# A state-space scan on one core: products issued ahead of their scans, named PSUM slots, and conv and projection pieces in other steps

## The chip, the cores and the metric

The kernel runs on one core of a Trainium2 chip. The time is device microseconds from the first to the last instruction of the program, as a median over runs. One execution was also recorded by the hardware profiler; all durations of instructions come from that one. The core has five engines that run their own instruction queues in order: TensorE (PE; its weight loads are listed as PEld), VectorE (DVE), ScalarE (ACT), GpSimd (POOL), and SyncE (SP), which here only issues DMAs.

## The reference

The input is 32 images of 96 channels and 56 x 56 pixels, all float32. Two layers follow one another:

- Layer 0 is a ConvNeXt block: a 7 x 7 depthwise convolution, a normalisation over channels, a product with w1 (96 to 384), GELU, a product with w2 (384 to 96), and the residual.
- Layer 1 reads the 3136 pixels of an image as a sequence and runs two Mamba blocks over it. Each block normalises, projects to x and z (192 channels each), applies a causal convolution of 4 taps and silu to x, computes from it `delta`, `B` and `C` (16 states), and then the recurrence, for each channel and each state,

```
h[t] = exp(delta[t] * A) * h[t-1] + delta[t] * B[t] * x[t]
y[t] = sum over states of C[t] * h[t]  + D * x[t]
```

  y is multiplied by silu(z), projected to 96 channels and added. After both blocks come a pooled branch, a fusing product, a batch normalisation over all images, and the residual.

## The kernel before, in words

**Tiling.** A sequence is cut into 4 chunks of 784 tokens, each in two halves of 392. A *stage* is one chunk of one image in one of the two Mamba blocks: 32 x 4 x 2 = 256 stages, in the list `stages`. Within a stage the 192 channels x 16 states are cut into 24 *steps*: group j (0 to 5) has 32 channels, quarter g (0 to 3) has 4 states, and a step works on 128 partitions (32 channels x 4 states) x 784 tokens. Step r of a stage has j = r // 4 and g = r % 4; n counts steps over all stages.

**A step.** It needs four things:

- `exps` (L869): ACT computes exp(delta * A). For an *unpooled* group (j = 0, 1, 3, 4) the result goes into an SBUF tile `da` (11 buffers), two steps ahead (`lead`, L882). For a *pooled* group (j = 2 and 5) it goes into PSUM, one step ahead.
- the product delta * x * B. For an unpooled group, `spread` (L886) has PE copy u = delta * x of 32 channels onto 128 partitions in a PSUM tile `u4` (two banks), and DVE multiplies by B just before the scan (L921), into a second PSUM tile `w`, or, for quarter 3, into `u4` in place. For a pooled group POOL multiplies instead (`pooled`, L899), in SBUF, from a copy of u that a DMA spread; those eight products of a stage are placed in steps 0, 2, 4, 6 and 12, 14, 16, 18.
- the scan on DVE (L928), which writes one of four slots of the ring `h`.
- the product with C on POOL (L932), into the `da` tile of the step. Three steps later PE sums this over states into the PSUM tile `y` (`add_up`, L948). After the second group of a pair, `gate` (L943) has DVE multiply y by silu(z). For steps 4 and 12 (`LATE`) the gate is issued between the product and the scan.

The slots for `u4`, `w` and the exponentials of pooled groups all come from one PSUM tag with two buffers of two banks (`wide`, L865).

**What runs beside it.** The order of every engine's instructions is that of the program; it is written by hand. Each piece of other work has a slot, a step number with a fraction: `put` (L973) files it and `run` issues all pieces of a step, by fraction, after the step's scan (those marked True in between, ahead of the scan). A slot below 0 or over 24 falls into a neighbouring stage. The pieces are:

- `prep` (L587): for the next stage, the normalisation (steps 11 to 15), the input projections (`project`, with the x weights in three thirds q = 0, 1, 2 from step 16 on, then `silu("xc")`, the z projections and `silu("z")`), `dbl` and `dt` (delta, B, C) and the DMAs that spread them. Its slots are the list `t` (L752), to which 0.1 is added.
- `post` (L784): output projection of the stage before, from step 7.5.
- `block0` (L400): half a chunk of layer 0 of a later image, steps 11 to 18, with `pool` and `fuse` once an image.
- `conv` (L534): the depthwise convolution of a pair of channels for 5 images, as products with a band matrix: two parts of 7 taps each (3 images and 2), each ended by ACT's copy and a DMA (`store`). There are 192 of them, one a stage.

All of these pieces use three PSUM tiles of one bank, `ps0`, `ps1`, `ps2` (`psum(k)`, L346). [...]

Of the kernel before, what the change touches and what calls it, by code (L numbers as in the profile page):

```python
# [34 lines left out]
F32 = mybir.dt.float32  # L35
I32 = mybir.dt.int32
AF = mybir.ActivationFunctionType
ALU = mybir.AluOpType
# [10 lines left out]
NG = 4  # L49
DTR = 6  # L50
NX = DTR + 2 * NS
NCH = 4
CH = L // NCH
HC = CH // 2
# [7 lines left out]
def convnext_mamba_kernel(  # L62
# [31 lines left out]
    nc = tc.nc  # L94
# [249 lines left out]
    with ExitStack() as main:  # L344
# [12 lines left out]
        def halves(t):  # L357
            return t.rearrange("p (a b) -> p a b", a=2)
# [41 lines left out]
        def block0(b, c, s):  # L400
            k = c * 2 + s
            v = {}

            def load():
                if k == 0:
                    batch_sums[b] = work([C, NCH * 2], "sums", 2)
                v["cv"] = work([C, ROWS, W], "cv", 1)
                g = 0 if b < b0 else 1 + (b - b0) // NB
                at = (b - groups[g][0]) * W
                nc.sync.dma_start(  # L410
                    v["cv"],
                    conv_d[g].rearrange("(c h) w -> c h w", h=H)[
                        :, k * ROWS : (k + 1) * ROWS, at : at + W
                    ],
                )

            def load_x():
                if s == 0:
                    xins[b, c] = work([C, CH], "xin", 1)
                    nc.sync.dma_start(xins[b, c], x[b, :, c * CH : (c + 1) * CH])  # L420

            def center():
                v["cv"] = v["cv"].rearrange("p r w -> p (r w)")
                v["ps"] = centred(v["cv"], 2)

            def square():
                v["sq"] = squared(v["ps"])

            def mean():
                v["ps"] = mean_of(v["sq"], 2)  # L430

            def root():
                if pre and s == 0:
                    exp_ln_tables()
                rsqrt(v["ps"])

            def norm():
                nc.vector.tensor_tensor(hn0s[s][0:C], v["cv"], v["ps"][0:C, 0:HC], ALU.mult)

            def up():  # L440
                v["pss"] = [psum(f) for f in range(NF)]
                for f in range(NF):
                    nc.tensor.matmul(
                        v["pss"][f][:, 0:HC], w1_sb[:, f * 128 : (f + 1) * 128], hn0s[s],
                        start=True, stop=True,
                    )

            def gelu():
                v["gl"] = work([128, NF, HC], "gl", 1)
                for f in range(NF):  # L450
                    nc.scalar.activation(
                        v["gl"][:, f], v["pss"][f][:, 0:HC], AF.Gelu, bias=b1_sb[:, f : f + 1]
                    )
                if not pre:
                    exp_ln_tables()

            def down():
                v["ps"] = psum(2)
                nc.tensor.matmul(
                    v["ps"][0:C, 0:HC], eye, xins[b, c][:, tok(s)], start=True, stop=False  # L460
                )
                for f in range(NF):
                    nc.tensor.matmul(
                        v["ps"][0:C, 0:HC], w2_sb[:, f, :], v["gl"][:, f, :],
                        start=False, stop=(f == NF - 1),
                    )

            def residual():
                xs = xins[b, c][:, tok(s)]
                nc.scalar.activation(  # L470
                    xs, v["ps"][0:C, 0:HC], AF.Identity, bias=b2ls,
                    accum_out=batch_sums[b][:, k : k + 1],
                )
                if s == 1:
                    nc.sync.dma_start(x1_d[b][:, c * CH : (c + 1) * CH], xins.pop((b, c)))


            def total():
                v["m"] = work([C, 1], "mean", 2)
                nc.vector.tensor_reduce(v["m"], batch_sums[b], AX.X, ALU.add)  # L480

            def pool():
                ps = psum(2)
                nc.tensor.matmul(ps[0:C, 0:1], gpw_sb, v["m"], start=True, stop=True)
                v["gp"] = work([C, 1], "gp", 2)
                nc.scalar.activation(v["gp"], ps[0:C, 0:1], AF.Relu, bias=gpb, scale=1.0 / L)

            def fuse():
                ps = psum(2)
                nc.tensor.matmul(ps[0:C, 0:1], fw2, v["gp"], start=True, stop=True)  # L490
                fb = (
                    const.tile([C, 1], F32, name="fb0")
                    if pre
                    else wp.tile([C, 1], F32, name="fb", tag="fb", bufs=3)
                )
                nc.scalar.activation(fb, ps[0:C, 0:1], AF.Identity, bias=fusb)
                batch_bias[b] = fb

            last = [(21.5, total), (29.9, pool), (30.9, fuse)] if k == 2 * NCH - 1 else []
            return last + [  # L500
                (-6, load), (2, load_x), (11.3, center), (12.1, square), (12.4, mean),
                (12.8, root), (14.1, True, norm), (15.6, up), (15.9, gelu), (17.3, down),
                (18.3, residual),
            ]
# [29 lines left out]
        def conv(g, p):  # L534
# [24 lines left out]
            def store(part):  # L559
# [11 lines left out]

                return piece

            at = (7.7, 8.2, 8.6, 9.2, 9.6, 10.2, 10.4), (18.5, 18.6, 19.2, 20.2, 21.2, 21.3, 22.2)
            return [
                (-1, load), (11.05, store(0)), (22.9, store(1)),
                *[(at[part][dw], tap(part, dw)) for part in range(2) for dw in range(7)],
            ]

# [7 lines left out]
        def prep(S):  # L587
# [161 lines left out]
                (-18, load), (-12.9, center), (-11.9, square), (-11.8, halo), (-11.6, mean),  # L749
                (-11.2, root), (-9, True, norm),  # L750
            ]
            t = (-7.6, -7.5, -6.5, -6, 0, 0.1, 1, 2.3, 3.1, 3.4, 4)  # L752
            if S in (stages[2], stages[-1]):

                start = [
# [106 lines left out]
        convs = [(g, p) for g in range(1, len(groups)) for p in range(C // 2)]  # L862
        halfs = [(b, c, s) for b in range(1, B) for c in range(NCH) for s in range(2)]

        def wide():  # L865

            return pu.tile([128, 1024], F32, name="w", tag="w", bufs=2)

        def exps(n):  # L869

            m, r = divmod(n, NSTEP)
            if m == len(stages):
                return
            S, j, g = stages[m], r // NG, r % NG
            if j in POOLED:
                e = wide()[:, 0:CH]
            else:
                e = S.da[j, g] = wp.tile([128, CH], F32, name="da", tag="da", bufs=11)
            nc.scalar.activation(e, S.d4[j], AF.Exp, scale=S.d["A"][:, j, g : g + 1])  # L879
            S.e[j, g] = e  # L880

        def lead(n):  # L882

            return 1 if n % NSTEP // NG in POOLED else 2

        def spread(n):  # L886

            m, r = divmod(n, NSTEP)
            if m == len(stages) or r // NG in POOLED:
                return  # L890
            S, j = stages[m], r // NG
            S.u4 = wide()
            for a in range(2):
                nc.tensor.matmul(  # L894
                    S.u4[:, 512 * a : 512 * a + HC], sel[rows(a), j % 2, :],
                    S.u[rows(a), j // 2, :], start=True, stop=True,
                )

        def pooled(m, j, g):  # L899


            def piece():
                S = stages[m]
                t = S.da[j, g] = wp.tile([128, CH], F32, name="da", tag="da", bufs=11)
                nc.gpsimd.tensor_tensor(t, S.us[j], S.bcs[g][:, 0, :], ALU.mult)  # L905

            return piece

        def scan(n):
            m, r = divmod(n, NSTEP)  # L910
            S, j, g = stages[m], r // NG, r % NG
            d, c = S.d, S.c
            da = S.da[j, g]
            if j in POOLED:
                db = da
            else:

                if g == 0:
                    S.w = wide()
                db = (S.u4 if g == NG - 1 else S.w)[:, 0:CH]  # L920
                nc.vector.tensor_tensor(  # L921
                    halves(db), S.u4.rearrange("p (a b) -> p a b", a=2)[:, :, 0:HC],
                    halves(S.bcs[g][:, 0, :]), ALU.mult,
                )
            if r in LATE and n >= NSTEP // 3:
                gate(n - LAG - 2)
            run(n, within)
            nc.vector.tensor_tensor_scan(  # L928
                ring[:, g, :], S.e.pop((j, g)), db, 0.0 if c == 0 else d["st"][:, j, g : g + 1],
                ALU.mult, ALU.add,  # L930
            )
            nc.gpsimd.tensor_tensor(da, ring[:, g, :], S.bcs[g][:, 1, :], ALU.mult)  # L932
# [54 lines left out]
        for m, S in enumerate(stages):  # L987
# [3 lines left out]
                put(m, [(NG * (j - 2) + 2 * g, pooled(m, j, g)) for g in range(NG)])  # L991
            if 2 <= m < len(halfs) + 2:
                put(m, block0(*halfs[m - 2]))
            if 2 <= m < len(convs) + 2:
                put(m, conv(*convs[m - 2]))
            if m + 1 < len(stages):
                put(m, prep(stages[m + 1]))
        put(len(stages), post(stages[-1]))
# [129 lines left out]
```

## Time and profile before

| | |
|---|---|
| median of 3 runs | 17278.04 us (17271.47 to 17292.32) |
| profiled execution, span | 17284.9 us |
| the program around the span | starts and ends with it: nothing is counted outside |
| stages | 559 to 16917 us; ahead of them weights and the first convolutions, after them the batch normalisation |
| one stage | 63.7 us (2259 scans between 3000 and 9000 us) |
| busy | DVE 93%, POOL 91%, PE 90%, ACT 66% |

A line of the profile's groups gives source line, engine, operation, what it writes and reads with shapes, how often, then the busy time in us and the mean of one in ns, and after the next bar the engine's idle time just before these instructions with what ended most of it. A line of the timeline gives start and length in us, and in brackets the engine's idle time before it. Ends of matmuls are modelled, so PE's busy time is not PE at its peak.

### The profile page before, as it was taken

To read this page: it belongs to the slowest core of one execution; us is meant where nothing else is said; L and a number is where in the kernel's file an instruction comes from. 1 tells how busy PE (TensorE), PEld (TensorE's weight loads), DVE (VectorE), ACT (ScalarE), POOL (GpSimd) and SP (SyncE) were. 2 spreads that over 40 slices of the span, in tenths; PEclk is the share of its full clock that TensorE was granted. 3 is DMA by queue.
4 is the path that set the end of the run, shared out by engine and by line. 5 is a ranking of instruction groups with operands and counts; after the bars stand their busy time and mean duration, and the time that the engine had idled before them with its cause. 6 is when DMAs were issued, how large, how long until landed. Compare 5 with 4: busy or idle time off the path is not lost. (4 is left out here: it accounts for less than half of the span.)

```text
span 17284.9 us, 207580 instructions
## 1 busy us (share of the span) xinstructions
PE 15488.9 (90%) x69336; PEld 5550.7 (32%) x69336; DVE 16068.6 (93%) x12351; ACT 11452.6 (66%) x18723; POOL 15673.1 (91%) x8798
## 2 busy tenths in 40 slices
PE   8899999999999999999999999999998888888870
PEld 5333333333333333333333333333332222222220
DVE  8699999999999999999999999999999999999994
ACT  1666676666666676666667667676666666666653
POOL 1699999999999999999999999999999999999991
PEclk9899999999999999999999999999999999999985
DMA  4344444444444444444444444444443433333338
GB/s 112 115 133 138 137 139 137 135 138 137 139 132 137 139 138 139 133 137 138 139 133 139 139 138 140 132 139 137 139 137 121 130 128 123 128 127 129 122 117 276
DMA packets 1303114, 2362.16 MB, mean 137 GB/s; under 512 B 516398, under 2 KB 669242, under 8 KB 1302040
## 3 DMA queue, kind: packets, MB, share of 16 engines
q1 hardware_dynamic: 1292712, 2308.46, 42.1%
q10 hardware_dynamic: 7168, 38.54, 0.6%
q8 instruction: 547, 8.96, 0.2%
q14 instruction: 527, 4.32, 0.1%
q0 software_dynamic: 2160, 1.88, 0.1%
HBM read 1945.97 MB, written 402.41 MB: 136 GB/s over the span
## 5 line engine op out<-in xcount | busy, mean ns | idle before, releaser
L932 POOL TENSOR_TENSOR da<-h,bc 128x784 f32<-128x784 f32 x6144 | 11302.5, 1863 | 749.6 <-DVE h L928 656.6
L928 DVE TENSOR_TENSOR_SCAN h<-da,st,w 128x784 f32<-128x784 f32 x3072 | 5666.0, 1844 | 319.9 <-ACT st L939 4.6
L965 PE MATMUL y<-da,ssum 128*32 128x392 f32 x24576 | 5126.1, 535 | 373.0 <-POOL da L932 372.6
L921 DVE TENSOR_TENSOR w<-w,bc 128x784 f32<-128x784 f32 x4096 | 3997.2, 976 | 229.5 <-PE w L894 58.5
L905 POOL TENSOR_TENSOR da<-us,bc 128x784 f32<-128x784 f32 x2048 | 3822.2, 1866 | 0.0
L879 ACT ACTIVATE da<-d,A 128x784 f32<-128x784 f32 x4096 | 3763.7, 941 | 31.4 <-DMA d<-dd 15.4
L879 ACT ACTIVATE w<-d,A 128x784 f32<-128x784 f32 x2048 | 1878.5, 918 | 2658.9 <-DVE h L928 2607.9
L928 DVE TENSOR_TENSOR_SCAN h<-w,st,da 128x784 f32<-128x784 f32 x1536 | 2712.6, 1828 | 5.9 <-ACT w L879 4.8
L633 PE MATMUL ps<-hn,wx 97*64 97x392 f32 x12288 | 2265.0, 503 | 7.3 <-DVE hn L621 7.3
L965 PEld LDWEIGHTS y<-da,ssum 128*32 128x32 f32 x24576 | 1069.2, 114 | 3428.6 <-issue 1968.3
L928 DVE TENSOR_TENSOR_SCAN h<-da,w 128x784 f32<-128x784 f32 x1024 | 1827.0, 1784 | 104.5 <-DVE w L921 1.0
L894 PE MATMUL w<-u,sel 64*128 64x392 f32 x4096 | 1021.0, 577 | 624.3 <-DVE h L928 623.2
L633 PEld LDWEIGHTS ps<-hn,wx 97*64 97x64 f32 x12288 | 796.3, 137 | 1432.1 <-issue 1097.4
L712 POOL TENSOR_TENSOR u<-dl,xc 128x784 f32<-128x784 f32 (+1 forms) x512 | 739.1, 1444 | 468.7 <-ACT dl L698 468.7
L552 PE MATMUL ps<-xpad,band 112*112 112x168 f32 (+1 forms) x5376 | 1087.1, 312 | 0.0
L552 PEld LDWEIGHTS ps<-xpad,band 112*112 112x112 f32 x5376 | 710.3, 175 | 1088.3 <-issue 1025.7
L959 PE MATMUL y<-xc,D 128*128 128x392 f32 x1536 | 792.7, 602 | 254.5 <-DVE z L946 249.4
L368 ACT ACT_TABLE_LOAD x759 | 973.8, 1283 | 14.1 <-PEq L1115 0.8
L377 ACT ACTIVATE sq<-ps 96x392 f32<-96x392 f32 x768 | 344.5, 490 | 823.6 <-PE ps L372 397.0
L928 DVE TENSOR_TENSOR_SCAN h<-w,da 128x784 f32<-128x784 f32 x512 | 872.4, 1766 | 0.0
L690 PE MATMUL ps<-dbl,dtw 6*64 6x392 f32 x3072 | 676.9, 506 | 99.4 <-ACT dbl L668 99.4
L894 PEld LDWEIGHTS w<-u,sel 64*128 64x128 f32 x4096 | 325.9, 195 | 1138.8 <-DVE h L928 1011.6
(151 smaller groups left out, 14448.7 us busy)
## 6 DMA issues: line engine op xcount, KB each, us to landing
bc<-bd SPq DMA_DIRECT2D x2048, 392.0 KB, 6.3
d<-dd SPq DMA_DIRECT2D x1536, 392.0 KB, 3.9
us<-uu SPq DMA_DIRECT2D x512, 392.0 KB, 3.4
dd<-dl SPq DMA_DIRECT2D x512, 294.0 KB, 3.8
band<-band_d SPq DMA_DIRECT2D x192, 343.0 KB, 4.5
uu<-u SPq DMA_DIRECT2D x1024, 49.0 KB, 1.6
cv<-conv_d SPq DMA_DIRECT2D x256, 147.0 KB, 3.4
xin<-in_x SPq DMA_DIRECT2D x128, 294.0 KB, 4.8
```

Of the source, the lines that this page charges most:

```text
L368: nc.scalar.preload_act_table_set("natural_log_exp_and_others")
L552: nc.tensor.matmul(v["ps"][0:R2, 0 : (last - first) * W], v["band"][:, dw, :], xpad[:, first:last, dw : dw + W], start=(dw == 0), stop=(dw ...
L633: nc.tensor.matmul(v["x", q][rows(a), 0:HC], weights[:, k, 64 * q : 64 * q + 64], v["hn"][:, o : o + HC], start=(k == 0), stop=(k == last),)
L712: nc.gpsimd.tensor_tensor(S.u[:, lo:hi], v["dl"][:, lo:hi], S.xc[:, lo:hi], ALU.mult)
L879: nc.scalar.activation(e, S.d4[j], AF.Exp, scale=S.d["A"][:, j, g : g + 1])
L894: nc.tensor.matmul(S.u4[:, 512 * a : 512 * a + HC], sel[rows(a), j % 2, :], S.u[rows(a), j // 2, :], start=True, stop=True,)
L905: nc.gpsimd.tensor_tensor(t, S.us[j], S.bcs[g][:, 0, :], ALU.mult)
L921: nc.vector.tensor_tensor(halves(db), S.u4.rearrange("p (a b) -> p a b", a=2)[:, :, 0:HC], halves(S.bcs[g][:, 0, :]), ALU.mult,)
L928: nc.vector.tensor_tensor_scan(ring[:, g, :], S.e.pop((j, g)), db, 0.0 if c == 0 else d["st"][:, j, g : g + 1], ALU.mult, ALU.add,)
L932: nc.gpsimd.tensor_tensor(da, ring[:, g, :], S.bcs[g][:, 1, :], ALU.mult)
L959: nc.tensor.matmul(S.y[:, 0:HC], S.d["D"][:, q, :], S.xc[:, q, :], start=True, stop=False)
L965: nc.tensor.matmul(S.y[r0 : r0 + 32, 0:HC], ssum, da[:, tok(a)], start=False, stop=(g == NG - 1),)
```

## The change

1. In `scan`, an unpooled group issues its products in pairs: at quarter 0 those of quarters 0 and 3, at quarter 1 those of 1 and 2. The product of quarter 3 goes into an SBUF `da` tile; its exponential goes into PSUM, one step ahead instead of two. The product of quarter 2 goes into `u4` in place. Gate and inner pieces come ahead of the products.
2. `wide` has two named slots, `w0` (u4, even pooled quarters) and `w1` (w, odd pooled quarters, the exponential of quarter 3).
3. In `t`, the last third of the input projection moves from slots 0.1 and 0.2 to -1.0 and -0.9, the silus and z projections from 1.1-1.3 to 0.1-0.3.
4. In `conv`, part 0 moves from 7.7-10.4 to 4.6-7.2 with its store at 7.5, part 1 from 18.5-22.2 to 7.9-10.4 with its store at 11.05. The convolutions start one stage later.
5. `pool` and `fuse` use `ps0` and `ps1` and move by half a step.

```diff
-                ps = psum(2)
+                ps = psum(0)
-                ps = psum(2)
+                ps = psum(1)
-            last = [(21.5, total), (29.9, pool), (30.9, fuse)] if k == 2 * NCH - 1 else []
+            last = [(21.5, total), (29.4, pool), (30.4, fuse)] if k == 2 * NCH - 1 else []
...
-            at = (7.7, 8.2, 8.6, 9.2, 9.6, 10.2, 10.4), (18.5, 18.6, 19.2, 20.2, 21.2, 21.3, 22.2)
+            at = (4.6, 5.2, 5.6, 6.2, 6.4, 6.6, 7.2), (7.9, 8.4, 8.8, 9.4, 9.7, 10.2, 10.4)
-                (-1, load), (11.05, store(0)), (22.9, store(1)),
+                (-1, load), (7.5, store(0)), (11.05, store(1)),
...
-            t = (-7.6, -7.5, -6.5, -6, 0, 0.1, 1, 2.3, 3.1, 3.4, 4)
+            t = (-7.6, -7.5, -6.5, -6, -1.1, -1, 0, 2.3, 3.1, 3.4, 4)
...
-        def wide():
-            return pu.tile([128, 1024], F32, name="w", tag="w", bufs=2)
+        def wide(k):
+            return pu.tile([128, 1024], F32, name=f"w{k}", tag=f"w{k}", bufs=1)
+        def in_psum(j, g):
+            return j in POOLED or g == NG - 1
+        def product_tile(S, j, g):
+            t = S.da[j, g] = wp.tile([128, CH], F32, name="da", tag="da", bufs=11)
+            return t
+        def times_b(S, out, g):
+            nc.vector.tensor_tensor(
+                halves(out), S.u4.rearrange("p (a b) -> p a b", a=2)[:, :, 0:HC],
+                halves(S.bcs[g][:, 0, :]), ALU.mult,
+            )
...
-            if j in POOLED:
-                e = wide()[:, 0:CH]
-            else:
-                e = S.da[j, g] = wp.tile([128, CH], F32, name="da", tag="da", bufs=11)
+            e = wide(g % 2)[:, 0:CH] if in_psum(j, g) else product_tile(S, j, g)
...
-            return 1 if n % NSTEP // NG in POOLED else 2
+            return 1 if in_psum(*divmod(n % NSTEP, NG)) else 2
...
-            S.u4 = wide()
+            S.u4 = wide(0)
...
-            da = S.da[j, g]
-            if j in POOLED:
-                db = da
-            else:
-                if g == 0:
-                    S.w = wide()
-                db = (S.u4 if g == NG - 1 else S.w)[:, 0:CH]
-                nc.vector.tensor_tensor(
-                    halves(db), S.u4.rearrange("p (a b) -> p a b", a=2)[:, :, 0:HC],
-                    halves(S.bcs[g][:, 0, :]), ALU.mult,
-                )
             if r in LATE and n >= NSTEP // 3:
                 gate(n - LAG - 2)
             run(n, within)
+            if j not in POOLED and g < 2:
+                if g == 0:
+                    S.w = wide(1)[:, 0:CH]
+                times_b(S, S.w, g)
+                if g == 0:
+                    times_b(S, product_tile(S, j, NG - 1), NG - 1)
+                else:
+                    times_b(S, S.u4[:, 0:CH], 2)
+            da = S.da[j, g]
+            db = da if in_psum(j, g) else S.u4[:, 0:CH] if g == 2 else S.w
             nc.vector.tensor_tensor_scan(
...
-            if 2 <= m < len(convs) + 2:
-                put(m, conv(*convs[m - 2]))
+            if 3 <= m < len(convs) + 3:
+                put(m, conv(*convs[m - 3]))
```

More of the change, by code (lines that the diff above doesn't have):

```diff
@@ L903, in piece @@
                 S = stages[m]
-                t = S.da[j, g] = wp.tile([128, CH], F32, name="da", tag="da", bufs=11)
-                nc.gpsimd.tensor_tensor(t, S.us[j], S.bcs[g][:, 0, :], ALU.mult)
+                nc.gpsimd.tensor_tensor(
+                    product_tile(S, j, g), S.us[j], S.bcs[g][:, 0, :], ALU.mult
+                )
             return piece
```

## The prediction

> **What bounds the kernel now.** A step r = 0..23 handles group j = r // 4 and quarter g = r % 4; S3 is the scan of step 3, P3 its product, M3 the GpSimd product that follows, Pd a pooled product. I read the page first, then the cut at mid-run, then each engine in order of time. The engines' busy shares:
>
> ```profile
> PE 15488.9 (90%) x69336; PEld 5550.7 (32%) x69336; DVE 16068.6 (93%) x12351; ACT 11452.6 (66%) x18723; POOL 15673.1 (91%) x8798
> ```
>
> Three engines stand at 90% or more, so shares don't name the bound. The groups on the two fullest:
>
> ```profile
> L932 POOL TENSOR_TENSOR da<-h,bc 128x784 f32<-128x784 f32 x6144 | 11302.5, 1863 | 749.6 <-DVE h L928 656.6
> L928 DVE TENSOR_TENSOR_SCAN h<-da,st,w 128x784 f32<-128x784 f32 x3072 | 5666.0, 1844 | 319.9 <-ACT st L939 4.6
> L921 DVE TENSOR_TENSOR w<-w,bc 128x784 f32<-128x784 f32 x4096 | 3997.2, 976 | 229.5 <-PE w L894 58.5
> L905 POOL TENSOR_TENSOR da<-us,bc 128x784 f32<-128x784 f32 x2048 | 3822.2, 1866 | 0.0
> ```
>
> POOL's idle time ends with a scan (656.6 of 749.6 us): POOL waits for DVE, while DVE's named waits are small. Next, the stretch from 3000 to 9000 us (length; PE, PEld, DVE, ACT, POOL busy; clock; DMA):
>
> ```profile
> 3000.00:9000.00 6000.00, 5624.99 (x25653) 2014.90 (x25654) 5730.49 (x4367) 4167.92 (x6882) 5749.33 (x3202) 0.96 0.43 137
> ```
>
> It holds 2259 scans, 94.1 stages: 63.74 us a stage, with 60.9 of DVE, 61.1 of POOL, 59.8 of PE, 44.3 of ACT. The rest of DVE's stage is no named wait; the order of time shows it (start, length):
>
> ```profile
> 8021.21 0.98 DVE L921 TENSOR_TENSOR w<-w,bc 128x784 f32<-128x784 f32 x1
> 8022.33 1.85 DVE L928 TENSOR_TENSOR_SCAN h<-da,st,w 128x784 f32<-128x784 f32 x1
> 8024.21 0.98 DVE L921 TENSOR_TENSOR w<-w,bc 128x784 f32<-128x784 f32 x1
> ...
> 8033.13 0.98 DVE L921 TENSOR_TENSOR w<-w,bc 128x784 f32<-128x784 f32 x1
> 8034.02 0.56 DVE L946 TENSOR_TENSOR z<-y,z 128x392 f32<-128x392 f32 x1
> ...
> 8045.10 7.05 DVE L928 TENSOR_TENSOR_SCAN h<-w,st,da 128x784 f32<-128x784 f32 x4
> ```
>
> A scan that reads the product just before it starts 1.12 us after the product's start (8021.21 to 8022.33); an instruction that doesn't depend on it starts after 0.89 (8033.13 to 8034.02). A product that overwrites what the scan reads starts 1.88 after the scan, an independent scan after 1.76 (four in 7.05). So DVE sets the pace, by its own pipeline: it is never late for others by more than fractions.
>
> POOL between its waits:
>
> ```profile
> 8015.84 10.96 POOL L932 TENSOR_TENSOR da<-h,bc 128x784 f32<-128x784 f32 x6
> 8026.76 1.84 POOL L905 TENSOR_TENSOR da<-us,bc 128x784 f32<-128x784 f32 x1
> ...
> 8063.60 1.86 POOL L932 TENSOR_TENSOR da<-h,bc 128x784 f32<-128x784 f32 x1 [2.55 <-DVE h L928]
> ```
>
> Six products take 10.92 start to start, 1.82 each. A stage has 24 M and 8 Pd (32 x 1.82 = 58.24) and two u products (8008.55 to 8010.36, 1.81; 8030.38 to 8031.36, 0.98): POOL's floor is **61.03 us**.
>
> ACT's silu burst, and TensorE's two clocks:
>
> ```profile
> 8022.98 1.28 ACT L646 ACT_TABLE_LOAD   x1
> 8024.27 1.54 ACT L646 ACTIVATE xc<-ps,cb 128x392 f32<-128x392 f32 x3
> ...
> 8028.52 1.28 ACT L368 ACT_TABLE_LOAD   x1
> 8029.82 1.79 ACT L879 ACTIVATE da<-d,A 128x784 f32<-128x784 f32 x2
> ```
>
> ```profile
> 8043.30:8050.10 6.80, 5.04 (x26) 2.19 (x25) 6.76 (x4) 3.83 (x6) 6.80 (x5) 1.00 0.37 116
> 8050.10:8056.90 6.80, 6.44 (x12) 2.70 (x12) 6.53 (x7) 3.48 (x8) 6.26 (x4) 0.50 0.96 346
> ```
>
> The burst holds ACT for 6.84 us. After a stretch with holes TensorE fell to half clock for 6.8 us.
>
> [...] The change keeps one operand of every product and scan in PSUM (quarter 3 swaps them: exponential in PSUM, product in SBUF), as pooled steps do already, at 1828 ns a scan against 1844; so I expect no slower POOL. [...]
>
> **The change, part by part.**
> *DVE.* An unpooled group becomes P0 P3 S0 P1 P2 S1 S2 S3. By the intervals above: 0.89 + 0.89 + (S0 to P1, which overwrites what S0 reads) 1.88 + 0.89 + 0.89 + 3 x 1.76 = 10.72. Before: group 0 8021.21 to 8033.13 = 11.92; group 1, 8033.13 to 8045.10 = 11.97 less the gate's 0.48 = 11.49; groups 3 and 4, taken likewise without norms, gate and stalls, 11.31 and 11.72. Sum 46.44 against 42.88: **-3.56 us** a stage. P3 into SBUF isn't in the trace; z<-y,z goes from PSUM to SBUF at 552 ns for half the columns, so nearest is 0 difference (bounds -0.05 to +0.1 each). DVE's own stage would be 63.74 - 3.56 = 60.2.
> *POOL* keeps every instruction: 61.03, so 0.85 above DVE. Of the 3.56 at most 63.74 - 61.03 = 2.71 can be gained.
> *Where DVE can't keep POOL fed.* The ring of 4 h slots makes S11 wait for M7. From there POOL has M8 to M15 and two Pd before M16: 10 x 1.82 = 18.2. DVE has S11 to S16 with gate 0.48, three norms 1.41, six products 5.34 and six scans 10.75 (S12 is 1.88, as a product overwrites its operand next): 18.0, plus two hand-overs of 0.1. No slack: a stall there is paid in full. I put it at 0.8 a stage: the product of step 12 waits for a later spread (below), and the norms wait for ACT. Bounds 0.2 (hand-overs only) to 2.
> *ACT.* Quarter 3's exponential moves from two steps ahead into PSUM, one ahead, after S1 has freed the slot. The silu burst moves from step 1 to 0 and now stands before that exponential. It starts 0.94 earlier (one exponential fewer before it), so ends at 8029.82 - 0.94 = P0 + 7.7 (P0 = 8021.21). S1 ends at P0 + 7.3; the exponential (0.92) is done at P0 + 8.65; S3 is due at P0 + 8.96. Cost 0, with 0.3 of cover; gone, each us of lateness is a us of stall, softened by what POOL has queued. Bounds 0 to 0.6. Steps 6, 14 and 18 have no burst in front but roots (14), which DVE waits for anyway. Gates issued ahead of products lose 0.89 of cover; y was added two steps before: 0 to 0.3.
> *PE.* No work is added. Input projection's last third moves from step 0 to 23, one y addition earlier; nothing costs. Conv's second seven taps (about 0.3 each, 2.1 us) move from steps 18 to 22 to steps 7 to 10, where PE before idled 1.2 us and waited for the scan before a spread. Between S23 and S11 PE has two spreads 1.7, twelve y additions 9.0, projections 4.9, dbl and dt 4.4, D 0.9, the output projection 3.65 and now 14 taps 4.8 instead of 7 with 2.7 (start to start in the trace): 29.4 instead of 27.3 us. DVE's time there shrinks from 31.04 (8019.34 to 8050.38) to 1.78 + 2 x 10.72 + 0.48 + 3 x 1.76 = 28.98: the spread of step 12 comes up to 1 us late, in my 0.8. In steps 20 to 22 only y additions stay.
> *Queues.* SP: the conv stores move from steps 11 and 22 to 7 and 11. Behind the first stand load_u (needed at step 12) and the B/C loads: 0. The d4 load of step 2 now waits for the late exponential, about 8029.8; behind it the B/C store, which left at 8032.38: hidden by 2.5 us. da tiles: P3's is taken a step before its exponential's was, at most 10 of 11 in use: 0; gone, DVE would wait for PE. Pool and fuse change PSUM tile and half a step, once in eight stages: 0. Convs start one stage later: 0.
>
> **Sum.** 61.03 + 0.2 + 0.8 = 62.0 a stage, 1.74 less. The second and the second-last stage, which prepare their successor in another order, take 77.6 and 78.1 us and I leave those: 254 x 1.74 = 442. Profiled 17284.9 - 442 = 16843; the median stands 7 us below its profile (17278.04), so **16836 us**.
>
> **The rivals.**
> 1. *TensorE becomes the bound.* It is 59.8 busy; every half-clock window costs up to 3.4 us, and until now 4 us of idle time took that up. With the taps in the crowded half, spreads and gates run late. Against: 62.0 still leaves it 2.2. Pitch 63.0: 17278 - 254 x 0.74 = **17090**.
> 2. *Slower: quarter 3's exponential behind the silu burst.* Steps 20 to 22 lose the taps, TensorE thins out, and the half clock falls on the projection and z matmuls (8022.19 to 8027.96: 5.06 us of work), so the burst ends up to 5 us later. It decides once S3 is over 2.7 us late in every stage. At 4.9: 60.2 + 4.9 = 65.1, **17620**; in two stages of three about 17360. Against: of the 203 half-clock windows of stages 10 to 189 none starts in steps 15 to 2, and with TensorE late these steps are dense.
> 3. *No change*: waits for gates and spreads take all that DVE frees: **17280**.
>
> **How the numbers follow.** A measurement tells 0.2% (35 us). POOL-paced (61.3 to 62.3, 16650 to 16910): 0.50. TensorE-paced (to 17240): 0.30. No change: 0.05. Slower: 0.15. The likeliest alone is 16650 to 16910; leaving out the slower case and the floor's last 20 us, the range is 16660 to 17235.
>
> **What would show it.** Right: two products 0.89 apart ahead of S0; POOL's idle time below 0.8 us a stage; DVE's waits named POOL; DVE busy share down, POOL at 96% or more. Wrong: scans of quarter 3 waiting for ACT w (rival 2), products or gates waiting for PE (rival 1), POOL products above 1.87 us[...].

## The result, and the profile after

| | before | after |
|---|---|---|
| median | 17280.6 us (17271.5 to 17292.3, 4 runs) | 17044.0 us (17029.6 to 17064.7, 4 runs) |
| profiled span | 17284.9 us | 17063.0 us |
| a stage with a convolution (stages 10 to 189, mean) | 63.71 us | 63.42 us |
| a stage without (200 to 251) | 64.17 us | 61.69 us |

The changed kernel takes 0.9865 of the time before (95% interval 0.9851 to 0.9879): 1.35% faster, 237 us. I had forecast 442. The last two rows say where the rest is (a stage is counted from the start of its first scan to that of the next stage's). The stages behind the last convolution gained 2.5 us each; the 192 with one gained 0.3. (The two stages with another order of preparation fell from 77.6 and 78.1 to 72.2 and 71.9 us.) The groups on the fullest engines, from the page:

```profile
L942 POOL TENSOR_TENSOR da<-h,bc 128x784 f32<-128x784 f32 x6144 | 11300.1, 1867 | 556.3 <-DVE h L938 436.9
L938 DVE TENSOR_TENSOR_SCAN h<-w,st,da 128x784 f32<-128x784 f32 x2304 | 4146.9, 1834 | 225.2 <-ACT st L949 92.8
L878 DVE TENSOR_TENSOR w<-w,bc 128x784 f32<-128x784 f32 x3072 | 2912.1, 978 | 279.5 <-PE w L905 191.5
L878 DVE TENSOR_TENSOR da<-w,bc 128x784 f32<-128x784 f32 x1024 | 988.0, 965 | 0.8 <-DMA bc<-bd 0.8
```

POOL is as fast as before (1867 ns against 1863), and the product into SBUF costs what the one into PSUM does (965 against 978 ns). What is new is that VectorE waits for others. Its waits between 3000 and 9000 us (in total, times, longest):

```profile
DVE z L956 <- PE y L975: 97.8, 123, 3.2
DVE w L878 <- PE w L905: 70.2, 83, 0.9
DVE h L938 <- ACT st L949: 60.5, 55, 2.3
DVE h L938 <- ACT w L890: 55.7, 106, 2.2
DVE h L938 <- POOL da L942: 14.0, 25, 2.3
```

In the kernel before, the same view's largest were these:

```profile
DVE hz L438 <- ACT ps L389: 20.0, 13, 2.1
DVE w L921 <- PE w L894: 16.2, 23, 0.9
DVE z L946 <- PE y L965: 16.1, 14, 1.2
```

VectorE now waits for TensorE's y (gates), TensorE's spread (products), and ScalarE (scans). The cut of that stretch:

```profile
3000.00:9000.00 6000.00, 5638.08 (x25787) 2033.15 (x25788) 5646.68 (x4391) 4181.64 (x6915) 5769.04 (x3218) 0.96 0.43 138
```

Over its 94.6 stages POOL idles 231 us, 2.44 us a stage; before it was 251 us over 94.1 stages, 2.66. So POOL hasn't become the bound in these stages. (Its busy share of 96% can't tell: it was 95.8% in the same cut before.)

One stage shows the chain. VectorE around steps 6 to 12, start and length:

```profile
6405.28 3.58 DVE L938 TENSOR_TENSOR_SCAN h<-da,st,w 128x784 f32<-128x784 f32 x2
6408.77 3.57 DVE L938 TENSOR_TENSOR_SCAN h<-w,st,da 128x784 f32<-128x784 f32 x2
6414.32 5.40 DVE L938 TENSOR_TENSOR_SCAN h<-w,st,da 128x784 f32<-128x784 f32 x3 [1.98 <-ACT st L949]
6420.36 0.57 DVE L956 TENSOR_TENSOR z<-y,z 128x392 f32<-128x392 f32 x1 [0.64 <-PE y L975]
6421.80 0.98 DVE L878 TENSOR_TENSOR w<-w,bc 128x784 f32<-128x784 f32 x1 [0.86 <-PE w L905]
6422.69 0.96 DVE L878 TENSOR_TENSOR da<-w,bc 128x784 f32<-128x784 f32 x1
6423.57 1.84 DVE L938 TENSOR_TENSOR_SCAN h<-da,st,w 128x784 f32<-128x784 f32 x1
```

The pair of products and its scan stand 0.89 and 0.88 apart (6421.80, 6422.69, 6423.57), as worked out. But the scan of step 9 came 1.98 late, the gate 0.64, the product 0.86. ScalarE at the first of these:

```profile
6408.89 0.92 ACT L890 ACTIVATE w<-d,A 128x784 f32<-128x784 f32 x1 [0.71 <-DVE h L938]
6413.01 0.40 ACT L565 ACTIVATE sq<-ps,cb 112x168 f32<-112x168 f32 x1 [3.20 <-PE ps L552]
6413.31 0.91 ACT L890 ACTIVATE w<-d,A 128x784 f32<-128x784 f32 x1
```

The copy of the convolution's part 0 waits 3.20 us for TensorE's last tap, and step 9's exponential stands behind it. (The view puts the scan's wait down to the copy `st` of line 949, which ends at the scan's own start, 6414.32; the exponential ended at 6414.22.) TensorE was late because of this:

```profile
6399.77 3.52 PE L690 MATMUL ps<-dbl,dtw 6*64 6x392 f32 x12 [0.60 <-ACT dbl L668]
6403.23 1.68 PE L969 MATMUL y<-xc,D 128*128 128x392 f32 x2
...
6412.43 0.54 PE L552 MATMUL ps<-xpad,band 112*112 112x168 f32 x2
...
6420.82 0.93 PE L905 MATMUL w<-u,sel 64*128 64x392 f32 x4
```

```profile
6402.00:6409.00 7.00, 7.00 (x19) 1.67 (x17) 6.96 (x6) 4.35 (x8) 7.00 (x4) 0.57 0.37 94
```

The product with D (line 969) took 1.68 us where it took 0.90 in the kernel before (at 8034.73, granted clock 1.00): from 6402 to 6409 the granted clock was 0.57, and from there TensorE is without a pause to the spread at 6420.82, as it has the convolution's second part in between. Call a stretch in which the granted clock is 0.50 a half-clock window. Over stages 10 to 189 of the changed kernel, the 153 with a window that starts at step 3 or 4 take 63.72 us and the 27 without take 61.70. Before the change it was 63.60 with (129 stages) and 64.01 without (51): the same windows were there and cost nothing.

The 153 are not alike. In 37 of them a second window starts at step 15; these take 65.87 us, and the gate after step 19 waits 2.36 us on average (1.22 to 3.20). The other 116 take 63.04. Measured against 61.70, either group loses some 155 us over these 180 stages, so half of the loss comes with the second window. Experiment 2 shows the same window in more stages.

Three theories for the missing half were tried; none of them named the second window. *Crowding*: the convolution's second part overfills TensorE's steps 23 to 10, and the half-clock window's loss is carried on until step 12. *Loop*: ring and POOL leave no slack, wherever the convolution stands. *Queue*: it is ScalarE's copy, waiting for a tap in front of an exponential.

### The profile page after: what moved, and what is told of

The parts are those of the page before. It is cut to its first block, busy times and chain, and to the rows that moved or that the text cites. A ratio compares the mean times of both kernels' runs of the same rounds, so it can differ in the third digit from the quotient of the medians.

```text
span 17063.0 us, 206746 instructions
## 1 busy us (share of the span) xinstructions
PE 15435.4 (90%) x69336; PEld 5562.9 (33%) x69336; DVE 15732.9 (92%) x12351; ACT 11443.3 (67%) x18723; POOL 15645.3 (92%) x8798
## 5 line engine op out<-in xcount | busy, mean ns | idle before, releaser
L942 POOL TENSOR_TENSOR da<-h,bc 128x784 f32<-128x784 f32 x6144 | 11300.1, 1867 | 556.3 <-DVE h L938 436.9
L975 PE MATMUL y<-da,ssum 128*32 128x392 f32 x24576 | 5258.9, 537 | 453.2 <-POOL da L942 428.8
L938 DVE TENSOR_TENSOR_SCAN h<-w,st,da 128x784 f32<-128x784 f32 x2304 | 4146.9, 1834 | 225.2 <-ACT st L949 92.8
L890 ACT ACTIVATE w<-d,A 128x784 f32<-128x784 f32 x3072 | 2801.6, 914 | 2104.8 <-DVE h L938 2068.5
L938 DVE TENSOR_TENSOR_SCAN h<-da,st,w 128x784 f32<-128x784 f32 x2304 | 4176.1, 1834 | 2.2 <-ACT st L949 2.2
L878 DVE TENSOR_TENSOR w<-w,bc 128x784 f32<-128x784 f32 x3072 | 2912.1, 978 | 279.5 <-PE w L905 191.5
L890 ACT ACTIVATE da<-d,A 128x784 f32<-128x784 f32 x3072 | 2830.9, 940 | 17.8 <-DMA d<-dd 14.8
L938 DVE TENSOR_TENSOR_SCAN h<-w,da 128x784 f32<-128x784 f32 x768 | 1339.7, 1775 | 115.4 <-ACT w L890 55.1
L938 DVE TENSOR_TENSOR_SCAN h<-da,w 128x784 f32<-128x784 f32 x768 | 1345.4, 1773 | 0.0
L878 DVE TENSOR_TENSOR da<-w,bc 128x784 f32<-128x784 f32 x1024 | 988.0, 965 | 0.8 <-DMA bc<-bd 0.8
L690 PE MATMUL ps<-dbl,dtw 6*64 6x392 f32 x3072 | 723.5, 530 | 145.1 <-ACT dbl L668 145.1
```

The source lines that it names most:

```text
L878: nc.vector.tensor_tensor(halves(out), S.u4.rearrange("p (a b) -> p a b", a=2)[:, :, 0:HC], halves(S.bcs[g][:, 0, :]), ALU.mult,)
L938: nc.vector.tensor_tensor_scan(ring[:, g, :], S.e.pop((j, g)), db, 0.0 if c == 0 else d["st"][:, j, g : g + 1], ALU.mult, ALU.add,)
L975: nc.tensor.matmul(S.y[r0 : r0 + 32, 0:HC], ssum, da[:, tok(a)], start=False, stop=(g == NG - 1),)
```

## The experiments

**1. The convolution back in its old steps**

```diff
-            at = (4.6, 5.2, 5.6, 6.2, 6.4, 6.6, 7.2), (7.9, 8.4, 8.8, 9.4, 9.7, 10.2, 10.4)
+            at = (7.7, 8.2, 8.6, 9.2, 9.6, 10.2, 10.4), (18.5, 18.6, 19.2, 20.2, 21.2, 21.3, 22.2)
-                (-1, load), (7.5, store(0)), (11.05, store(1)),
+                (-1, load), (11.05, store(0)), (22.9, store(1)),
```

> The changed kernel with both parts of the convolution back in their old steps (7.7 to 10.4 and 18.5 to 22.2, stores 11.05 and 22.9). Crowding theory (TensorE's steps 23 to 10 got more work than VectorE leaves time for, and a half-clock window at step 3 or 4 makes it late until step 12): the stages with convolutions fall from 63.4 to about 62.2 us, as against 61.7 without any; time about 16,810 us, and the waits before the scan of step 9 and the product of step 12 go. Loop theory (ring and GpSimd leave no slack, wherever the convolution stands): 17,020 to 17,060 us, no different from the changed kernel.

Measured: 16785.7 us, 0.9718 of the kernel before (0.9703 to 0.9732); 61.82 us a stage with a convolution. VectorE's waits and the cut between 3000 and 9000 us:

```profile
DVE w L878 <- PE w L905: 107.1, 181, 1.1
DVE h L938 <- ACT w L890: 35.1, 96, 0.5
DVE hz L438 <- ACT ps L389: 30.2, 40, 2.0
DVE z L956 <- PE y L975: 12.5, 34, 2.3
```

```profile
3000.00:9000.00 6000.00, 5677.06 (x26471) 2054.84 (x26470) 5776.09 (x4505) 4288.13 (x7092) 5922.73 (x3303) 0.97 0.44 141
```

The waits for gates are gone from 97.8 to 12.5. POOL idles 77 us in 97.1 stages, 0.80 a stage, and its busy time a stage is 61.0: this kernel runs at POOL's floor plus 0.8, close to the 62.0 that I had forecast for the whole change. Crowding holds; the loop theory as a cause of the missing half falls. The wait before step 9's scan is gone; the one before step 12's product is not quite (0.30 us a stage, 0.75 in the whole change), and the first product of a stage now waits 0.79. Half-clock windows at step 3 or 4 are as frequent (137 of 180 stages), and cost nothing again (61.79 with, 61.92 without). No window starts at step 15.

**2. Only part 1 back in its old steps** (part 0 stays in 4.6 to 7.2, store 7.5; part 1 as in experiment 1, store 22.9)

> The changed kernel with part 1 of the convolution alone back in steps 18 to 22, part 0 left in steps 4 to 7. Crowding theory: about as with both back, 16,780 to 16,850 us, since the same 2.1 us of matmuls leave the crowded half; the scan of step 9 no longer waits. Loop theory: 17,020 to 17,060 us.

Measured: 17108.5 us, 0.9903 (0.9888 to 0.9918). Neither theory had this: the taps had left the crowded half, and the kernel was slower than the whole change. The wait that grew is that of the gate after step 19: 192.1 us in the same stretch, against 97.8. That wait, one such gate in order of time, and TensorE before it:

```profile
DVE z L956 <- PE y L975: 192.1, 70, 3.5
```

```profile
6023.45 0.57 DVE L956 TENSOR_TENSOR z<-y,z 128x392 f32<-128x392 f32 x1 [3.17 <-PE y L975]
```

```profile
6006.87 0.93 PE L905 MATMUL w<-u,sel 64*128 64x392 f32 x4 [2.65 <-DVE hn L619]
6007.73 0.96 PE L975 MATMUL y<-da,ssum 128*32 128x392 f32 x4
6008.62 4.29 PE L443 MATMUL ps<-hz,w_sb 97*128 97x392 f32 x6
```

```profile
6002.30:6005.70 3.40, 1.93 (x10) 0.38 (x8) 3.40 (x4) 3.29 (x7) 3.40 (x3) 1.00 0.94 375
6005.70:6009.10 3.40, 2.23 (x9) 0.95 (x10) 3.40 (x5) 2.77 (x3) 3.00 (x3) 0.89 0.38 125
6009.10:6012.50 3.40, 3.40 (x6) 1.37 (x5) 3.29 (x4) 1.18 (x2) 3.22 (x2) 0.50 0.00 0
```

TensorE came to the spread of step 16 early and waited 2.65 us, until the scan of step 14 had read the slot (it ends at 6006.72; the view names a short `hn` instruction beside it); the granted clock then fell to 0.50, and six matmuls took 4.29 us where the same six took 2.24 at a clock of 1.00 (in the kernel before, at 8065.15). This wait, in step 14, is 2.49 us a stage here, 1.54 in the whole change and 1.27 in experiment 1. That it grew because TensorE has nothing to do in steps 8 to 10 is my reading; experiment 3 tests the hole and not what made it. The records have such a window starting at step 15 in 116 of 180 stages. Those take 64.84 us, the other 64 take 61.46.

**3. Filling that hole** (experiment 2 and, in step 14, two products whose result nobody reads)

```diff
+            def fill():
+                ps = psum(2)
+                for _ in range(2):
+                    nc.tensor.matmul(
+                        ps[0:C, 0:HC], center_m, v["cv"], start=True, stop=True
+                    )
...
+                *([] if pre else [(14.5, fill)]),
```

> The changed kernel with part 1 back in steps 18 to 22 (17,108 us) and two products more in step 14 whose result nobody reads (some 1.3 us of TensorE, in its idle time before the spread of step 16). Half-clock theory (that kernel is slow because 0.64 half-clock windows a stage start at step 15 and make the gate after step 19 2.1 us late): the windows at step 15 become rare and the time falls to 16,780 to 16,880 us although TensorE has more to do. Work theory (the taps and the last third of the projection are simply too much in steps 18 to 23): no better, 17,100 to 17,250 us.

Measured: 16761.6 us, 0.9697 (0.9683 to 0.9712): 2% faster than the same kernel with less work. No window starts at step 15 any more, in any of the 180 stages, and the wait in step 14 is down from 2.49 to 0.28 us.

```profile
DVE z L963 <- PE y L982: 6.6, 25, 0.3
```

That is VectorE's wait for gates in the same stretch, 192.1 without the filling. The half clock is what made experiment 2 slow. The amount of work isn't. The same filling in the whole change, with its 37 windows at step 15, was not run.

**4. Only the moves, the products as before**

> The kernel before with all moves of the change (convolution, input projection, silu, pool and fuse) but each product still just ahead of its scan. Crowding theory: VectorE's path is as long as before, and the late spreads and gates come on top: 17,330 to 17,450 us. Loop theory: VectorE still sets the pace and nothing is waited for: 17,260 to 17,300 us.

Measured: 17396.6 us, 1.0075 (1.0058 to 1.0092). VectorE's waits:

```profile
DVE w L921 <- PE w L894: 98.3, 76, 2.1
```

The product of step 12 waits for the spread (16.2 in the kernel before). In the stages with a half-clock window at step 3 or 4 a stage takes 64.54, in the others 62.90. No window starts at step 15 here. By themselves the moves cost 126 us, as crowding says, and without the second window.

**5. Only the products and slots, nothing moved**

> The kernel before with the products issued ahead and the two named slots, and no piece moved. The silu burst now stands in step 1 and ends about 1 us later, so the exponential of step 3 is some 0.7 us late in each stage. Crowding theory: still faster than the whole change, about 16,950 us, since the convolution isn't in the crowded half. Loop theory: slower than the whole change by the late exponential, 17,080 to 17,150 us.

Measured: 16957.8 us, 0.9818 (0.9803 to 0.9832), and 62.59 us a stage: the crowding theory's time.

```profile
DVE h L938 <- ACT w L890: 151.4, 103, 1.7
DVE w L878 <- PE w L905: 113.2, 137, 1.1
```

Here the silu burst stands in step 1, and step 3's scan waits 1.48 us a stage (idle time before it, over stages 10 to 189), about twice the 0.7 that I had put down; with the burst moved, in the whole change, it waits 0.30. So in three steps from the kernel before (17270.6 beside these runs): products and slots -313 us (16957.8), then projection, silu and the small moves -172 (16785.7, experiment 1), then the convolution's move +258 (17044.0).

**6. The copy of part 0 behind the exponential** (store at 8.1 instead of 7.5, part 1's first tap at 8.2)

> The changed kernel with the first convolution part's copy and store at 8.1 instead of 7.5, so that ScalarE computes the exponential of step 9 before it waits for TensorE's last tap; part 1 starts at 8.2. If ScalarE's wait for the tap is what costs (queue theory): the 0.9 us before the scan of step 9 goes, and with it 0.7 to 0.9 us of each of 192 stages: 16,870 to 16,910 us. If TensorE's lateness itself costs (crowding theory): the wait only moves on to the gate and the product of step 12, 16,990 to 17,050 us.

Measured: 17035.1 us, 0.9858 (0.9844 to 0.9873), the same as the whole change. So ScalarE's queue alone isn't the cause at this place. There is no profile of this run: that the wait moved on to step 12, as the crowding theory has it, isn't shown.

**7. Part 1 with two taps of seven** (five of the seven products for two of five images are left out)

> The changed kernel with part 1 of the convolution reduced to its first and last tap (five of seven products of these two images are left out, some 1.45 us of TensorE in steps 8 to 10; store and ScalarE's copy stay). Crowding theory: the time falls nearly as with the part moved away, to 16,790 to 16,880 us. Queue theory: only what comes before the scan of step 9 matters, and that was late before any of these taps: 17,000 to 17,050 us.

Measured: 16845.1 us, 0.9747 (0.9731 to 0.9764), 62.24 us a stage. Some 1.45 us less for TensorE in steps 8 to 10 (an estimate; two of these taps take 0.57 from start to start at 6417.53 in the changed kernel) gave 1.2 us a stage: crowding again. This is the change itself without the disputed work, so the stores and the place of part 0 aren't what costs most of the difference. It doesn't tell the two losses apart: no window starts at step 15 any more, and by the stages of the whole change (65.87 against 63.04 in 37 of 180) that is some 0.58 of the 1.18 us, an estimate. In experiment 1 too both go together. The kernel is still 59 us above experiment 1; its waits name the normalisation of step 14:

```profile
DVE hz L438 <- ACT ps L389: 81.8, 80, 2.9
```

and the records a window that starts at step 13 in 64 of 180 stages (62.79 us with it, 61.94 without), where experiment 1 has 15.

**8. Part 1 ending a step earlier than of old** (experiment 1, part 1 at 18.5, 18.6, 19.2, 19.6, 20.2, 20.6, 21.2, store at 21.9)

> The changed kernel with part 0 in its old steps and part 1 from step 18.5 to 21.2 with its store at 21.9, one step earlier than of old, so that the spread for the next stage's first group isn't behind the last taps. Crowding theory: the 0.8 us that the first product waits for that spread falls to about 0.2, 16,640 to 16,740 us as against 16,786 with the old steps. Loop theory: GpSimd is at its floor of 61.03 us plus 0.8 anyway, 16,770 to 16,800 us.

Measured: 16915.3 us, 0.9787 (0.9773 to 0.9802), worse than experiment 1 and a miss. VectorE's first wait, and ScalarE's second:

```profile
DVE h L938 <- ACT w L890: 202.1, 98, 2.4
...
DVE w L878 <- PE w L905: 21.6, 52, 1.1
```

```profile
ACT sq L565 <- PE ps L552: 334.5, 129, 3.4
```

The product does get its spread in time (21.6 against 107.1), but the copy at 21.9 waits for the taps in front of step 23's exponential, and that scan waits 2.1 us a stage. Here the queue theory is the explanation, and it has its own test:

**9. The same with the copy at 22.0**, one place further back in ScalarE's queue

```diff
-                (-1, load), (11.05, store(0)), (21.9, store(1)),
+                (-1, load), (11.05, store(0)), (22.0, store(1)),
```

> The kernel with part 1 from step 18.5 to 21.2 (16,915 us) with its copy and store at 22.0 instead of 21.9: ScalarE then computes the exponential of step 23 before it waits for the last tap. Queue theory: the 2.1 us a stage before the scan of step 23 goes and the product of the next step 0 still has its spread in time; 62.6 less up to 1.6 (GpSimd's floor of 61.03 plus 0.2 to 0.5) is 61.2 to 61.6 a stage, 16,620 to 16,740 us, below all others. Crowding theory alone: TensorE is late there anyway, and the wait moves to the spread, 16,780 to 16,920 us.

Measured: 16759.9 us, 0.9696 (0.9683 to 0.9710); 61.79 us a stage with a convolution.

```profile
DVE w L878 <- PE w L905: 95.6, 192, 1.1
DVE h L938 <- ACT w L890: 38.2, 99, 1.4
```

The wait for exponentials fell from 202.1 to 38.2: a tenth of a step in the order of one queue is worth 155 us. Part of it turned into the wait for the spread (21.6 to 95.6), so the time lies between the two forecasts, 20 us above the queue theory's and 20 us below the crowding theory's. This and experiment 3 are the fastest, 1.7% below the change; between them (16,759.9 and 16,761.6) there is no difference, and from experiment 1 it is 0.15%.

## Why the prediction was right or wrong

- *The range and its middle*: 17044 lies inside 16660 to 17235, but that range spans two mechanisms. The one that I held likeliest, POOL-paced (0.50, 16650 to 16910), holds in the stages without a convolution; in the 192 others VectorE waits for TensorE, to which I gave 0.30. The middle missed by 208 us, so the range held by its width and not by the mechanism that I put first. My own signs say so: pairs stand 0.89 apart, but POOL idles 2.44 us a stage and not below 0.8, only 14.0 us of VectorE's waits name POOL, and products and gates wait for PE. (The range's low end is 10 us above 16650, not the 20 that I wrote; nothing hangs on it.)
- *What bounds the kernel, and VectorE's intervals*: right. Pairs stand 0.89 apart; products and slots alone took off 313 us.
- *POOL's floor of 61.03 us*: right. Experiments 1, 3 and 9 sit at 61.7 to 61.8 a stage, with POOL idle 0.80 in the first of them, and stages without a convolution at 61.69 in the changed kernel. POOL's products are no slower (1867 ns against 1863), as I had expected with one operand in PSUM; that this is the reason was not tried.
- *"Where DVE can't keep POOL fed ... I put it at 0.8 a stage"*: this is the mis-sized term. In the stages with a convolution the pitch is 63.42 - 61.03 = 2.39 above POOL's floor; without the 0.2 that I had apart, that is 2.2 and not 0.8, just above my upper bound of 2. Where it comes from shows in VectorE's idle time before step 9's scan, step 12's product and the gates of 12 and 20: 0.83 + 0.75 + 0.45 + 0.56 = 2.6 us a stage. A pitch of 62.0 was met by 62 stages of 254 (61.69) and missed by 1.4 in the other 192: 192 x 1.4 = 269 us. The two odd stages, which I had left as they were, gave back 11.6.
- *The working of that term*: I had set 29.4 us of TensorE's work against 29.0 us at full clock and allowed 1 us. The half-clock windows were in the trace (129 of 180 stages had one at step 3 or 4) and I put their price into rival 1, where it belonged into the sum: before, TensorE had idle time behind them to catch up in (1.08 us between the window's end and the scan of step 12, a mean of the 129 stages); the convolution's second part filled it (0.00 in the 153 of the changed kernel). The second window, at step 15, I had not foreseen at all in this term; it makes half of the loss.
- *Rival 1, TensorE becomes the bound*: its time of 17090 was nearer than mine, and its mechanism is what experiments 1, 4 and 7 show for the first half of a stage (the window at step 15 adds to it in the whole change). Its "late spreads and gates" are the first two lines of VectorE's waits.
- *Queues: "the conv stores ... 0"*: I had costed SP's queue, where that holds, and not ScalarE's, in which the copy stands in front of exponentials. In the change it cost nothing of its own (experiment 6); in experiment 8 it cost 155 us.
- *Rival 2, slower by the silu burst*: did not happen; step 3's scan waited 0.30 us a stage, inside the 0 to 0.6 given. The move of the burst was worth having (1.48 without it). Its premise was half right: steps 15 to 2, free of half-clock windows before, got some at step 15 in 37 of 180 stages, and those take 65.87 us; but they made gates late, and not the burst.

## What to carry to other kernels

When one engine's path is shortened until three stand at the same length, a work list by engine is not enough: add up what the others have to do between two meeting points, and put in the loss that they until now made good in idle time. Moving work into an engine's hole can be right or wrong by where the next hole is; in experiment 2 a hole on TensorE cost twice, once as idle time (2.49 us a stage) and once as half clock behind it (64.84 us for a stage with the window at step 15, 61.46 without), and in experiment 3 useless products in it paid (17108.5 to 16761.6 us). Ask of each moved copy which instruction stands behind it in its engine's queue: between experiments 8 and 9 one place in ScalarE's was worth 155 us.

## What the runs showed of the hardware that was not expected

- Two useless products a stage (some 1.3 us, an estimate: one of this shape takes 0.66 from start to start at 6423.07 in the changed kernel) made a kernel 2% faster (17108.5 to 16761.6): the half-clock windows at step 15, in 116 of 180 stages without them, are gone.
- The windows come back at the same steps: in the changed kernel 153 of 180 stages have one that starts at step 3 or 4. They come on a fixed grid (their starts lie within 0.03 us of one) and last 3.41 us or a multiple of it: in the changed kernel 187 last 3.41, 137 last 6.83, 8 last 10.24 and 3 last 13.65, beside one long one at the end. In experiment 2 the 116 stages with a window at step 15 took 64.85 us within 0.25, which is 19 times 3.413, and 62 of the other 64 took 61.44 within 0.15, which is 18 times; in experiment 3 the stages lie between 61.4 and 61.7 (10th to 90th percentile). That a stage of a whole number of windows meets the same window again is my estimate from these lengths and was not tried.
- TensorE was partly busy in the stretches ahead of the windows named here. On the grid, the two stretches of 3.41 us ahead of the one in experiment 2 (it starts at 6008.35) had TensorE busy 2.70 and 1.48 us by the modelled ends; the 37 at step 15 in the changed kernel follow on a stretch with 1.59 busy. The one at 6401.24 follows on 2.81 busy, in part with matmuls whose operands have 6 partitions (line 690). What sets a window off was not tried.
